# A selective scan, attention and routed experts in one kernel: disjoint scatter views, sums on TensorE, one table set, a new order of partitions, and an earlier gather

## The chip, the cores and the metric

The kernel runs on one core of a Trainium2 chip. All data is float32. The metric is the device time of one execution in microseconds (us). Before the change the median of three runs is 3942.65 us (3942.25 to 3942.79).

A core has five engines that run their own instruction streams in order and wait for each other by semaphores: PE (TensorE: weight load and matmul), DVE (VectorE), ACT (ScalarE), POOL (GpSimd) and SP (which here only issues DMAs). Sixteen DMA engines move data between DRAM and the on-chip memory, whose 128 partitions are its rows.

## The reference

The input `x` is (4, 384, 32, 32): four images, 384 channels, 1024 positions. Cut to what matters:

```python
# layer 0: four directions k; state size 16; each (image, k, channel, state) is a recurrence over 1024 positions
x_dbl = einsum('bkdl,kcd->bkcl', cross_scan(groupnorm(x)), x_proj_weight)
dts, Bs, Cs = split(x_dbl)                         # 12, 16, 16 rows
dt = softplus(einsum('bkrl,kdr->bkdl', dts, dt_projs_weight) + dt_projs_bias)
h = h * exp(dt * A) + (dt * u) * B                 # step by step over l
y = sum over the 16 states of h * C  (+ D * u)
x = x + gelu(layernorm(merge of the four directions of y))
# layer 1, on tokens t = x as (4, 1024, 384)
t = t + causal_attention(layernorm(t))             # one head of width 384
g = top 2 of softmax(layernorm(t) @ gate_w)        # 4 experts, renormalised
t = t + sum over the 2 of g_e * (gelu(ln(t) @ w1[e] + b1[e]) @ w2[e] + b2[e])   # 384 -> 1536 -> 384
```

## The kernel before, in words

**Units and ticks.** The scan is cut into 768 units (192 per image). A unit is 32 channels times 4 states, which fill the 128 partitions, times 1024 positions. A Python loop over ticks `t` writes out the order of the instructions for every engine: one unit a tick, and beside it pieces of all other work, which are generators that yield "wait n ticks" or "this took PE about n us". So the order within each engine is fixed when the kernel is built.

**One unit.** `decay` (ACT, L606): `da = exp(dt * a)`. `front` (DVE, L613): `v = du * B` into PSUM. `middle` (DVE, L619): the recurrence as one scan instruction. `back` (POOL, L636): `h * C`, ordered to run beside the scan of the next unit. After four units `row` (PE, L661) sums the four states of each channel with the 0/1 matrix `sel` and adds into `y`. `ahead` makes DVE wait, once the first image is done, until buffers that it will need are free: there are 7 buffers of `h`.

**The order of partitions.** Partition p holds channel p // 4 and state p % 4 of its unit. Hence three broadcast loads, all issued by SP: `dt` and `du` (`spread_dt`, L574) read 32 rows of DRAM, each for 4 partitions in a row; `bc` (`spread_bc`, L585, once for B and once for C) reads 4 rows, the four of them 32 times over. Each is 128 rows of 4096 bytes.

```python
src = dts_d[u["b"], u["k"]][which, g * DJ : (g + 1) * DJ, :]
src = bass.AP(tensor=src.tensor, offset=src.offset, ap=[src.ap[0], [0, NI], src.ap[1]])   # dt, du
src = bass.AP(tensor=src.tensor, offset=src.offset, ap=[[0, DJ], *src.ap])                # bc
```

An `ap` lists [step, count] from the slowest dimension to the fastest; NI is 4, DJ is 32. `dt` is fetched 5 ticks ahead of its unit, `du` and `bc` 3 ticks. `dt` and `du` have four buffers each and serve 16 units (four groups of states); `bc` has two buffers, each for four units.

**The first image** has no attention or experts beside it. For part of its units `feed` and `turned` make `v` on ACT (L901) and PE (L923) in place of DVE: 104 of the 192.

**Softplus.** `project_dt` (once for each of 6 parts of an image) computes `dt` with two Exp and two Ln on ACT (L448, L450), and one tick later DVE bounds it (`bounded`, L454) and multiplies (L491). Exp and Ln are in different table sets of ACT, so each change costs an ACT_TABLE_LOAD.

**Routing and experts.** After attention each image's 1024 tokens go through `ready` in two halves of 4 chunks of 128 tokens: gates, top 2, and a place for each token in the lists of its two experts. Then 8 indirect DMAs a half, issued by POOL (L1319), scatter the token rows into `xs_d`. All write to the one tensor `xs_d`, so each waits for the one before it to land. `experts` runs 11 blocks of 256 tokens (L1483: 384 to 1536, L1521: 1536 to 384) with weights loaded by SP (L1416), and stores into `ys_d`. `combine` and `joined` gather each token's two rows (POOL, L1562), scale and add them on DVE (L1577), add the bias term by a small matmul and DVE (L1582, L1585), turn the result on PE (L1590) and store it.

**What overlaps.** Attention, routing and experts of image b run beside the scan of image b + 1. The last image's run alone after the last unit (the tail).

Of the kernel before, what the change touches and what calls it, by code (L numbers as in the profile page):

```python
# [16 lines left out]
P = 128  # L17
B = 4
# [36 lines left out]
def hybrid_kernel(  # L55
# [67 lines left out]
    class Shared:  # L123
# [24 lines left out]
    banks = Shared(  # L148
        FIRST_BANKS,
        lambda i, name: (ps_m if i < FIRST_BANKS else pools["pm"]).tile(  # L150
            [P, 512], F32, tag=f"pm{i}", name=name
        ),
        0,
    )
# [4 lines left out]
    def bank(name):  # L159

        ps = banks.now(name)
        banks.give(name)
        return ps

# [11 lines left out]
    ys_d = [dram.tile([E * CAP, C], F32, tag=f"ys_{i}", name=f"ysd_{i}") for i in range(1)]  # L176
    g_d = dram.tile([P, M, C], F32, tag="g", name="g_d")
# [17 lines left out]
    for i in range(NI):  # L195
        nc.scalar.dma_start(a_raw[i::NI], a_logs.rearrange("(g d) n -> d g n", d=DJ))
# [27 lines left out]
    state_i = const.tile([P, NI], F32, tag="state_i", name="state_i")  # L224
# [8 lines left out]
    dump = const.tile([P, 1], F32, tag="dump", name="dump")  # L233
# [10 lines left out]
    fresh = const.tile([P, E, 4], F32, tag="fresh", name="fresh")  # L244
    nc.gpsimd.memset(fresh, 1.0)
    nc.gpsimd.memset(fresh[:, :, 0:1], 0.0)
# [8 lines left out]
    nc.scalar.activation(a_raw, a_raw, AF.Exp)  # L255
    nc.scalar.activation(dump, eps, AF.Sqrt)

    def scan_weights():
        nc.vector.tensor_reduce(state_i, ident.rearrange("p (d i) -> p i d", i=NI), AX.X, ALU.add)
        nc.vector.tensor_scalar_mul(state_i, state_i, -1.0)  # L260
        nc.vector.memset(a4, 0.0)
        for i in range(NI):
            nc.vector.scalar_tensor_tensor(
                a4, a_raw.rearrange("p g (q i) -> p g q i", i=NI)[:, :, :, i],
                state_i[:, i : i + 1], a4, ALU.mult, ALU.add,
            )
        nc.vector.tensor_reduce(sel, ident.rearrange("p (d i) -> p d i", i=NI), AX.X, ALU.add)
# [90 lines left out]
    def groupnorm(b, u):  # L358
# [3 lines left out]
        if b > 0:  # L362
            var_c = sm.tile([P, M], F32, tag="gn_vc", name=f"gn_vc_{b}")
            sq = yield from slots.take(f"gn_sq_{b}", P, L)
            for m in range(M):
                nc.scalar.activation(
                    sq, u[m], AF.Identity, scale=-1.0 / L, accum_out=mean_c[:, m : m + 1]
                )
                yield "wait", 1
            for m in range(M):  # L370
                nc.scalar.activation(
                    sq, u[m], AF.Square, bias=mean_c[:, m : m + 1], accum_out=var_c[:, m : m + 1]
                )
                yield "wait", 1
# [26 lines left out]
        nc.scalar.activation(rstd, ps, AF.Sqrt, bias=eps)  # L401
# [4 lines left out]
        for m in range(M):  # L406
# [4 lines left out]
            else:  # L411
                nc.scalar.activation(
# [32 lines left out]
    def softplus(xs, logs):  # L445

        for x_, log in zip(xs, logs):
            nc.scalar.activation(log, x_, AF.Exp)  # L448
        for log in logs:
            nc.scalar.activation(log, log, AF.Ln, bias=1.0)  # L450
# [5 lines left out]
    def project_dt(b, pair, m, u, xd):  # L456
# [12 lines left out]
        for h in range(NH):  # L469
# [12 lines left out]
            for i, k in enumerate(ks):  # L482
                nc.scalar.activation(
# [4 lines left out]
        yield "wait", 1  # L488
# [15 lines left out]
    def first_dt(u, xd):  # L504
# [9 lines left out]
        for (i, h), ps in pss.items():  # L514
            nc.scalar.activation(
                dts[i][:, bass.ts(h, 512)], ps, AF.Identity, bias=dtb[:, ks[i], 0:1]
            )
# [17 lines left out]
    def preparation(b):  # L535
# [8 lines left out]
        if b == 0:  # L544
            nc.scalar.activation(dump, eps, AF.Exp)
# [21 lines left out]
    def spread_dt(n, which, tag):  # L567
# [5 lines left out]
        src = bass.AP(tensor=src.tensor, offset=src.offset, ap=[src.ap[0], [0, NI], src.ap[1]])  # L573
# [4 lines left out]
    def spread_bc(n):  # L578
# [3 lines left out]
        for j in range(2):  # L582
            src = rows_d[u["b"], u["pair"]][u["i"], j, u["q"] * NI : (u["q"] + 1) * NI, :]
            src = bass.AP(tensor=src.tensor, offset=src.offset, ap=[[0, DJ], *src.ap])
# [17 lines left out]
    def decay(n):  # L602
# [3 lines left out]
        u["decay"] = nc.scalar.activation(  # L606
# [84 lines left out]
    def layernorm(dst, src, name, lag):  # L691
# [29 lines left out]
        for h in range(n):  # L721
            for c in range(M):
                s = bass.ts(h, 512)
                nc.scalar.activation(sqs[c][:, s], dst[:, c, s], AF.Square)
# [14 lines left out]
        nc.scalar.activation(  # L739
# [28 lines left out]
    def fold():  # L768
# [36 lines left out]
        for m in range(M):  # L805
# [7 lines left out]
            nc.scalar.activation(g[:, m, :], ps[:, :C], AF.Copy, scale=-scale)  # L813
# [25 lines left out]
    def feed():  # L839
# [21 lines left out]
        for n in range(0, IMAGE, EACH):  # L861
# [19 lines left out]
            for q in range(NQ):  # L881
                n0 = n + q * NJ
                if n0 // NJ % 5 not in (1, 3, 4) or clock[0] > n0 - AHEAD:
# [9 lines left out]
                for h in range(2):  # L893
# [5 lines left out]
                    for t in range(4):  # L899
                        for i in range(NI):  # L900
                            nc.scalar.activation(  # L901
                                st[:, 4 * h + t, :].rearrange("p (d i) -> p i d", i=NI)[:, i, :],
                                ps[h][:, t * P : (t + 1) * P], AF.Copy,
# [25 lines left out]
    def finish(b):  # L929
# [8 lines left out]
        for m in range(M):  # L938
            nc.scalar.activation(
# [11 lines left out]
    def scaled_tokens(b, yb):  # L951

        sqs = []
        for c in range(M):
            sq = yield from slots.take(f"sq_at_{b}_{c}", P, L)
            nc.scalar.activation(sq, yb[:, c, :], AF.Square)
# [17 lines left out]
        nc.scalar.activation(flat, var[:, NH * P : 2 * NH * P], AF.Square)  # L974
# [3 lines left out]
        nc.scalar.activation(rs, rs, AF.Sqrt, bias=eps)  # L978
# [28 lines left out]
    def attention(b, yb, fx0):  # L1007
# [66 lines left out]
        def softmax(i, ss, pr):  # L1074
# [8 lines left out]
            for n, (o, e, ps) in enumerate(ss):  # L1083
                nc.scalar.activation(  # L1084
# [6 lines left out]
        def normalise(i, nb, n):  # L1091
# [4 lines left out]
            nc.scalar.activation(prs[i][:, :wd], prs[i][:, :wd], AF.Copy, scale=nb[:, 2:3])  # L1096

        def turn(i):
# [14 lines left out]
            slots.give(f"pr_{b}_{i}")  # L1113

        moments = sm.tile([P, NB, 2], F32, tag="moments", name=f"moments_{b}")

        def values(i):
# [14 lines left out]
            def rows():  # L1132
# [8 lines left out]
                if i % 4 == 3:  # L1141
                    h = i // 4
                    if h == 1:
                        rt = routes[b] = Route(b)
                    rows_ = fx0 if h == 0 else routes[b].rows
                    defer(1, lambda: side.append(ready(b, h, yb, rows_, moments)))
# [22 lines left out]

    def ready(b, h, yb, rows, moments):  # L1170

        name = f"{b}_{h}"
        mean, rstd = moments[:, 4 * h : 4 * h + 4, 0], sm.tile([P, 4], F32, tag="rstd", name=f"rstd_{name}")
        shift = sm.tile([P, 4], F32, tag="shift", name=f"shift_{name}")
        nc.scalar.activation(rstd, moments[:, 4 * h : 4 * h + 4, 1], AF.Sqrt, bias=eps)
# [4 lines left out]
        chunks = [yb[:, :, bass.ts(4 * h + q, P)] for q in range(4)]  # L1180
        xts = []
        for q in range(4):
            nc.scalar.activation(
                rows[:, q, :].rearrange("p (m t) -> p m t", m=M), chunks[q], AF.Identity,
                bias=shift[:, q : q + 1], scale=rstd[:, q : q + 1],
# [3 lines left out]
        if h == 1:  # L1189
            held.clear()  # L1190
        pg = yield from banks.take(f"pgate_{name}")
        for q in range(4):
# [7 lines left out]
            yield "pe", 0.5  # L1200
            yield "wait", 1
            nc.scalar.copy(xt[:, q % 2, :], ps[:, :C])
            banks.give(f"pxt_{name}_{q}")
            xts.append(xt[:, q % 2, :])
        yield "wait", 1
        for q in range(4):
# [5 lines left out]
        yield "pe", 2.6  # L1212
        slots.give(f"xt_{name}_0", f"xt_{name}_2")
        yield "wait", 1
        sc = sm.tile([P, 4, E], F32, tag="sc", name=f"sc_{name}")
        nc.vector.tensor_tensor(
            sc, pg[:, : 4 * E].rearrange("p (q e) -> p q e", e=E),
            gb.unsqueeze(1).to_broadcast([P, 4, E]), ALU.add,
# [4 lines left out]
        def over(v):  # L1223
            return v.unsqueeze(2).to_broadcast([P, 4, E])

        red = sm.tile([P, 4], F32, tag="red", name=f"red_{name}")
        nc.vector.tensor_reduce(red, sc, AX.X, ALU.max)
        nc.vector.tensor_tensor(sc, sc, over(red), ALU.subtract)
        nc.scalar.activation(sc, sc, AF.Exp)
# [4 lines left out]

        cmp = [one.tile([P, 4, E, E], F32, tag=f"cmp{i}", name=f"cmp{i}_{name}") for i in range(2)]
        each = sc.unsqueeze(3).to_broadcast([P, 4, E, E])
        other = sc.unsqueeze(2).to_broadcast([P, 4, E, E])
# [3 lines left out]
            cmp[1], cmp[1], lower.unsqueeze(1).to_broadcast([P, 4, E, E]), ALU.mult  # L1241
        )
        nc.vector.tensor_tensor(cmp[0], cmp[0], cmp[1], ALU.max)
        cnt = sm.tile([P, 4, E], F32, tag="cnt", name=f"cnt_{name}")
        nc.vector.tensor_reduce(cnt, cmp[0], AX.X, ALU.add)

        sel = sm.tile([P, E, 4], F32, tag="sel", name=f"sel_{name}")
        nc.vector.tensor_single_scalar(sel.rearrange("p e q -> p q e"), cnt, 1.5, ALU.is_lt)
        cum = sm.tile([P, E, 4], F32, tag="cum", name=f"cum_{name}")
        nc.vector.tensor_tensor_scan(  # L1250
            cum.rearrange("p e q -> p (e q)"), fresh.rearrange("p e q -> p (e q)"),
# [3 lines left out]
        mk = sm.tile([P, 4, E], F32, tag="mk", name=f"mk_{name}")  # L1255
        nc.vector.scalar_tensor_tensor(mk, cnt, 1.5, sc, ALU.is_lt, ALU.mult)
        nc.vector.tensor_reduce(red, mk, AX.X, ALU.add)
        nc.vector.tensor_scalar_add(red, red, 1e-9)
        nc.vector.reciprocal(red, red)
        nc.vector.tensor_tensor(mk, mk, over(red), ALU.mult)  # L1260

        counts[b, h] = cum
        pp = yield from banks.take(f"place_{name}")
        flat = pp[:, : 4 * E]
# [6 lines left out]
        if h == 1:  # L1271
            before = counts[b, 0][:, :, 3:4]
            nc.tensor.matmul(
                flat.rearrange("p (e q) -> p e q", e=E), ones, before.to_broadcast([P, E, 4]),
                start=False, stop=True,
            )
            for i in range(2):
                nc.tensor.matmul(
                    pp[:, 4 * E : 5 * E], ones, counts[b, i][:, :, 3], start=(i == 0), stop=(i == 1)
                )  # L1280
        yield "pe", 1.5
        pm = yield from banks.take(f"pm_{name}")
        for q in range(4):
            nc.tensor.transpose(pm[:E, q * P : (q + 1) * P], mk[:, q, :], ident)
        yield "pe", 0.5
# [6 lines left out]
        at = sm.tile([P, E, 4], F32, tag="at", name=f"at_{name}")  # L1292
        nc.vector.tensor_tensor(at, flat.rearrange("p (e q) -> p e q", e=E), base, ALU.add)
        spot = sm.tile([P, 4, 2], F32, tag="spot", name=f"spot_{name}")
        two = [sm.tile([P, E, 4], F32, tag=f"two{i}", name=f"two{i}_{name}") for i in range(2)]
# [479 lines left out]
```

## Time and profile before

The profiled execution took 3944.32 us, and its span from first to last instruction is 3942.6 us.

| stretch of the span, us | what runs | DVE busy | PE busy | DMA share | GB/s |
|---|---|---|---|---|---|
| 0 to 50 | groupnorm and projections of image 0 | 18.0 | 20.3 | 0.61 | 174 |
| 50 to 750 | scan of image 0 | 605.2 | 418.8 | 0.60 | 215 |
| 750 to 1634 | scan of image 1 | 792.3 | 702.1 | 0.64 | 224 |
| 1634 to 2511 | scan of image 2 | 782.8 | 687.9 | 0.62 | 216 |
| 2511 to 3341 | scan of image 3 | 773.3 | 661.7 | 0.60 | 209 |
| 3341 to 3488 | tail: layer norm, attention | 45.6 | 129.2 | 0.16 | 49 |
| 3488 to 3551 | tail: routing and scatters | 12.1 | 15.3 | 0.24 | 80 |
| 3551 to 3902 | tail: experts | 0.0 | 350.7 | 0.53 | 167 |
| 3902 to 3943 | tail: gathers, sums, stores | 14.0 | 19.4 | 0.56 | 164 |

Busy columns are microseconds within the stretch. The DMA share is the mean busy share of the 16 DMA engines. In the four scan stretches DVE is busy 86 to 93% of the time; in the last stretches other engines set the end.

### The profile page before, as it was taken

How to read it: one execution, taken by the hardware profiler on the slowest of the kernel's cores; microseconds unless marked ns; L12 is line 12 of the kernel's file. 1: busy time of each engine (PE TensorE's matmuls, PEld its weight loads, DVE VectorE, ACT ScalarE, POOL GpSimd, SP SyncE). 2: the span in 40 equal slices, each digit the busy share in tenths (PEclk: the TensorE clock that was granted, in tenths of full speed). 3: DMA queues.
4: the chain of work that ended last, by engine and by line, in shares of the span. 5: the costliest groups of instructions: out<-in, count | busy, mean ns of one | idle time of the engine just before them, and what ended most of it. 6: DMA issues, size and time to landing. Idle time of an engine off the chain costs nothing. (4 is left out here: it accounts for less than half of the span.)

```text
span 3942.6 us, 40290 instructions
## 1 busy us (share of the span) xinstructions
PE 3005.2 (76%) x12787; PEld 1745.6 (44%) x12787; DVE 3043.2 (77%) x2250; ACT 2093.9 (53%) x3244; POOL 1973.9 (50%) x929
## 2 busy tenths in 40 slices
PE   4566655779478889678559799678479997859997
PEld 1233333335145556234235566234146663537774
DVE  5888888999988888989898899999889999310001
ACT  5778888556465567346446566255245553322211
POOL 2576666645565555645554566755565666010001
PEclk7677777789689999789669999779589998869998
DMA  5557655454467778534457878543368876115554
GB/s 190 195 206 262 240 197 194 173 190 165 146 215 277 277 251 307 192 137 169 145 198 252 300 247 304 190 162 136 112 222 311 279 276 208 50 52 180 180 174 139
DMA packets 405154, 798.17 MB, mean 202 GB/s; under 512 B 47484, under 2 KB 278572, under 8 KB 404940
## 3 DMA queue, kind: packets, MB, share of 16 engines
q1 hardware_dynamic: 390540, 770.01, 56.2%
q0 software_dynamic: 8192, 25.17, 1.9%
q8 instruction: 102, 1.67, 0.2%
q10 hardware_dynamic: 6208, 0.39, 0.1%
q14 instruction: 112, 0.92, 0.1%
HBM read 680.44 MB, written 115.02 MB: 202 GB/s over the span
## 5 line engine op out<-in xcount | busy, mean ns | idle before, releaser
L636 POOL TENSOR_TENSOR h<-h,bc 128x1024 f32<-128x1024 f32 x768 | 1814.9, 2369 | 1306.9 <-DVE v L613 1146.0
L619 DVE TENSOR_TENSOR_SCAN h<-da,v 128x1024 f32<-128x1024 f32 x768 | 1748.9, 2283 | 49.7 <-PE v L923 18.0
L606 ACT ACTIVATE da<-dt,a 128x1024 f32<-128x1024 f32 x768 | 884.2, 1159 | 777.4 <-DVE h L619 668.5
L613 DVE TENSOR_TENSOR v<-du,bc 128x1024 f32<-128x1024 f32 x664 | 888.9, 1339 | 181.1 <-PE y L661 66.2
L661 PE MATMUL y<-h,sel 128*32 128x512 f32 x3072 | 612.3, 716 | 281.1 <-POOL h L636 271.8
L1483 PE MATMUL ph<-turned,w 128*128 128x256 f32 x3168 | 733.8, 390 | 83.9 <-DMA w<-in_w 81.5
L1521 PE MATMUL py<-w,ht 128*128 128x384 f32 x2112 | 702.6, 490 | 14.7 <-DMA w<-in_w 14.3
L1483 PEld LDWEIGHTS ph<-turned,w 128*128 128x128 f32 x3168 | 611.5, 196 | 213.2 <-issue 89.2
L1521 PEld LDWEIGHTS py<-w,ht 128*128 128x128 f32 x2112 | 398.2, 191 | 314.8 <-issue 31.6
L1491 ACT ACTIVATE ht<-ph,b1t 128x256 f32<-128x256 f32 x528 | 221.1, 470 | 590.4 <-PE ph L1483 551.0
L661 PEld LDWEIGHTS y<-h,sel 128*32 128x32 f32 x3072 | 108.2, 121 | 657.2 <-POOL h L636 427.0
L1577 DVE SCALAR_TENSOR_TENSOR z<-g,shares,z 128x384 f32<-128x384 f32 x64 | 60.8, 951 | 409.3 <-DMA g<-ysd,places 408.4
L1562 POOL DMA_INDIRECT g<-ysd,places x64 | 73.5, 1148 | 394.4 <-DMA z<-t2d 368.1
L923 PE MATMUL v<-ident,st 128*128 128x128 f32 x832 | 152.9, 346 | 145.9 <-DVE h L619 145.2
L901 ACT ACTIVATE st<-turn,bt 128x128 f32<-128x128 f32 x832 | 242.7, 544 | 0.1
L923 PEld LDWEIGHTS v<-ident,st 128*128 128x128 f32 x832 | 125.5, 180 | 186.3 <-DVE h L619 105.7
L1319 POOL DMA_INDIRECT xsd<-fx,places x32 | 39.7, 1240 | 204.8 <-ACT mt L1311 143.7
L454 DVE SCALAR_TENSOR_TENSOR dt<-du,dt 128x1024 f32<-128x1024 f32 x48 | 64.3, 1339 | 77.9 <-ACT du L450 68.3
L1126 PE MATMUL po<-vt,pt 128*128 128x384 f32 x288 | 110.0, 532 | 13.4 <-ACT pt L1024 13.3
L475 PE MATMUL pdt<-xd,wdt 12*128 12x512 f32 x184 | 86.5, 806 | 34.7 <-ACT st L901 13.9
L1449 PE MATMUL pxg<-ident,xg 128*128 128x128 f32 x264 | 40.0, 290 | 84.7 <-DMA xg<-xsd 84.7
L1063 PE MATMUL ss<-axn,qt 128*128 128x512 f32 (+3 forms) x288 | 101.2, 496 | 4.2 <-ACT pr L1084 3.2
(263 smaller groups left out, 2316.4 us busy)
## 6 DMA issues: line engine op xcount, KB each, us to landing
w<-in_w SPq DMA_DIRECT2D x528, 384.0 KB
bc<-rows SPq DMA_DIRECT2D x384, 512.0 KB
dt<-dts SPq DMA_DIRECT2D x192, 512.0 KB
du<-dts SPq DMA_DIRECT2D x192, 512.0 KB
dts<-dt SPq DMA_DIRECT2D x48, 512.0 KB
dts<-du SPq DMA_DIRECT2D x48, 512.0 KB
xg<-xsd SPq DMA_DIRECT2D x44, 384.0 KB
ysd<-yt SPq DMA_DIRECT2D x44, 384.0 KB
```

The lines of the kernel that those rows point to most:

```text
L606: u["decay"] = nc.scalar.activation(u["da"], spread["dt4", n], AF.Exp, scale=a4[:, g, u["q"] : u["q"] + 1])
L613: return nc.vector.tensor_tensor(u["v"], spread["du4", n], spread["bc", n][:, 0, :], ALU.mult)
L619: nc.vector.tensor_tensor_scan(u["h"][:, ::step], u["da"][:, ::step], u["v"][:, ::step], 0.0, op0=ALU.mult, op1=ALU.add,)
L636: product = units[n]["product"] = nc.gpsimd.tensor_tensor(h, h, spread["bc", n][:, 1, :], ALU.mult)
L661: units[n]["row"] = nc.tensor.matmul(y, sel, h, start=first, stop=last, tile_position=(0, jj * DJ))
L901: nc.scalar.activation(st[:, 4 * h + t, :].rearrange("p (d i) -> p i d", i=NI)[:, i, :], ps[h][:, t * P : (t + 1) * P], AF.Copy, scale=bt[ ...
L923: nc.tensor.transpose(u["v"][:, t * P : (t + 1) * P], st[:, t, u["j"] * P : (u["j"] + 1) * P], ident)
L1063: nc.tensor.matmul(ps[:, : e - o], qt[:, c, i * P : (i + 1) * P], xn[o // 512][:, c, : e - o], start=(c == 0), stop=(c == M - 1 and (alone ...
L1126: nc.tensor.matmul(po[:, :C], pts[i][:, j, :], vt[:, j, :], start=False, stop=(j == i))
L1483: nc.tensor.matmul(ps[:, i * BT : (i + 1) * BT], t[:, c, i * P : (i + 1) * P], xt[:, c, :], start=(c == 0), stop=(c == M - 1),)
L1491: nc.scalar.activation(ht[:, f + i, :], ps[:, i * BT : (i + 1) * BT], AF.Gelu if alone else AF.Identity, bias=biases[j][:, f + i : f + i + 1],
L1521: nc.tensor.matmul(pss[i][:, :C], hts[j][:, 2 * c + f, i * P : (i + 1) * P], t[:, f, :], start=(c == 0 and f == 0), stop=(c == 5 and f == 1),)
```

## The change

Five things are changed together.

1. **Scatters.** `dram_disjoint_views(xs_d[0], 16)` makes 16 views of the list tensor that are declared not to overlap; each scatter of an image writes through its own. The routing goes in three groups of 4, 2 and 2 chunks in place of two halves. In the last image no ticks lie between the scatters of a group.
2. **Sums.** `combine` no longer uses DVE: for each chunk ACT builds two diagonal matrices from the token's shares, and 12 matmuls of 128x128 add the residual, the bias term and the two scaled rows, already turned, in one PSUM tile.
3. **Tables.** All ACT functions go through `act`, which loads the set `natural_log_exp_and_others` for Exp and Ln alike. `project_dt` waits two ticks in place of one before DVE bounds the result.
4. **States 32 partitions apart.** Partition p now holds state p // 32 and channel p % 32. The broadcast loads, `a_raw`, `a4`, `sel` and the writes of `st` follow. `feed` asks for other units (three groups of four in place of three of five), of which 91 of 192 are made.
5. **The end.** For the last image the gather of each token's first row is issued after the last block but one (`early`), the second after the last block (`late`); four more PSUM tiles serve the tail (`more_banks`), and DVE copies half of each `yt`.

```diff
+    views = dram_disjoint_views(xs_d[0], 2 * L // P)
...
+    def act(dst, src, f, **more):
+        if f in KINDS:
+            tables_for(KINDS[f])
+        return nc.scalar.activation(dst, src, f, **more)
...
-        yield "wait", 1
+        yield "wait", 2
         for i, k in enumerate(ks):
             bounded(dts[i], dus[i])
...
-        src = bass.AP(tensor=src.tensor, offset=src.offset, ap=[src.ap[0], [0, NI], src.ap[1]])
+        src = bass.AP(tensor=src.tensor, offset=src.offset, ap=[[0, NI], *src.ap])
         nc.sync.dma_start(t, src)
...
-            src = bass.AP(tensor=src.tensor, offset=src.offset, ap=[[0, DJ], *src.ap])
+            src = bass.AP(tensor=src.tensor, offset=src.offset, ap=[src.ap[0], [0, DJ], src.ap[1]])
             nc.sync.dma_start(bc[:, j, :], src)
...
-                if n0 // NJ % 5 not in (1, 3, 4) or clock[0] > n0 - AHEAD:
+                if n0 // NJ % 4 == 0 or clock[0] > n0 - AHEAD:
                     continue
...
+    GROUPS = ((0, 4), (4, 2), (6, 2))
...
                 nc.gpsimd.indirect_dma_start(
-                    out=xs_d[0],
+                    out=views[2 * (q0 + q) + i],
...
+    def add_up(ps, g, z, terms, first, last):
+        for n, what in enumerate(terms):
+            for m in range(M):
+                s = bass.ts(m, P)
+                lhs, rhs = {
+                    "t2": (z[:, s], ident),
+                    "b2": (b2s[:, s], g[:E, 2 * C : 2 * C + P]),
+                    0: (g[:, m * P : (m + 1) * P], z[:, 2 * C : 2 * C + P]),
+                    1: (g[:, C + m * P : C + (m + 1) * P], z[:, 2 * C + P : 2 * C + 2 * P]),
+                }[what]
+                nc.tensor.matmul(ps[:, s], lhs, rhs, ...)
...
+    def early(b):
+        for i in range(L // P):
...
+            gather(b, i, g, 0)
+            beside(b, i, g, z)
+        yield "wait", 3
+        for i in range(L // P):
+            ps = yield from banks.take(f"pz_{b}_{i}")
+            add_up(ps, *closing[i], ("t2", "b2", 0), True, False)
...
+    def late(b):
+        for i in range(L // P):
+            gather(b, i, closing[i][0], 1)
+        for i in range(L // P):
...
+            add_up(ps, g, z, (1,), False, True)
+            put_out(b, i, ps, z)
```

## The prediction

> **What bounds the kernel now.** I read the windows by stage first (the table above), then the groups of instructions, then the waits, then the chain that ended last. The groups name the engine that bounds the scan:
>
> ```profile
> L636 POOL TENSOR_TENSOR h<-h,bc 128x1024 f32<-128x1024 f32 x768 | 1814.9, 2369 | 1306.9 <-DVE v L613 1146.0
> L619 DVE TENSOR_TENSOR_SCAN h<-da,v 128x1024 f32<-128x1024 f32 x768 | 1748.9, 2283 | 49.7 <-PE v L923 18.0
> L613 DVE TENSOR_TENSOR v<-du,bc 128x1024 f32<-128x1024 f32 x664 | 888.9, 1339 | 181.1 <-PE y L661 66.2
> ```
>
> POOL's 1146 us of idle time are spent waiting for DVE's `v`; DVE's scan has 49.7 us of idle time before it in all. So DVE sets the pace: a tick on DVE is 2.283 + 1.339 = 3.62 us (2.3 where `v` comes from ACT and PE), and 768 ticks fill 3291 us (50 to 3341), 4.3 us each. After 3341 the chain runs through PE, the scatters and the gathers. DVE's waits:
>
> ```profile
> DVE z L1577 <- DMA g<-ysd,places: 408.4, 9, 397.0
> DVE dt L454 <- ACT du L450: 68.3, 16, 7.3
> DVE v L613 <- PE y L661: 66.2, 26, 11.8
> DVE v L613 <- DMA du<-dts: 43.6, 24, 5.3
> DVE v L613 <- DMA bc<-rows: 18.9, 11, 4.8
> ```
>
> The first is the idle tail. DMA costs DVE some 62 us today, in 35 waits: the engines keep up. That depends on what part 4 of the change touches:
>
> ```profile
> q1 hardware_dynamic: 390540, 770.01, 56.2%
> ...
> bc<-rows SPq DMA_DIRECT2D x384, 512.0 KB
> dt<-dts SPq DMA_DIRECT2D x192, 512.0 KB
> du<-dts SPq DMA_DIRECT2D x192, 512.0 KB
> ```
>
> 768 broadcast loads of 128 rows of 4096 bytes are 402.7 of the 770 MB, all on SP's one queue.
>
> **Part 4, the order of partitions: the term that decides.** The loads keep their bytes and packets; the slowest dimension of the source falls from 32 to 4 (dt, du: 4 copies of 32 rows; bc: 4 rows of 32 copies). The trace has no such load of 4096-byte rows, but its semaphore records show how transfers are shared out: every load of 128 rows or 32 x 4 raises its semaphore in 16 updates; `wdt` loads of 12 rows give 13 (12 and one more), and `z<-gtd`, `gtd<-mt`, `b2s`, whose slowest dimension is 4 rows, give 5 (4 and one). So I read that a transfer whose slowest dimension counts 4 runs on 4 engines of the 16. The built instruction of the changed kernel still carries [32, 4] in this order.
>
> [...] The rows show the counts; which four engines, no run here shows. [...]
>
> Price, from the packet records: the 118,912 packets of 4096 bytes take 159 ns in the median and 181 ns in the mean (a tenth over 191). Now each of 16 engines has 8 packets of a load (1.3 to 1.4 us); on four, each has 32: 5.09 to 5.79 us a load. Identical shapes should make an identical choice, so I take the same four each time: 768 x 5.09 to 5.79 = 3908 to 4448 us on each, mid 4178. Their other work: the DMA share times the length of the four stretches is 0.60 x 700 + 0.64 x 884 + 0.62 x 877 + 0.60 x 830 = 2027 us per engine, of which the loads are 768 x 8 x 0.181 = 1112; 915 stay. So the four engines need 4823 to 5363 us for a scan that takes 3291, mid 5093: 6.6 us a tick against DVE's 3.62. I add 60 us (bounds 0 and 400): `dt` and `du` have four buffers each, freed only four ticks before the next group needs them, so 10 of the 16 loads of every 16 units fall into some five ticks, while in the others the loads can wait for buffers. Scan: about 5150 in place of 3291. If the four varied from load to load, two or three loads would share the 16 engines, only the delay to landing would grow (1.3 to 5.4 us, against a lead of 3 to 5 ticks, 11 us or more), and this term would be 0 to +200.
>
> Small: 26 groups of turned units become 23, 13 units more at 1.256 us (median of `v`): +16 on DVE. All that is below the DMA floor; it counts only if the loads stay fast.
>
> **Part 1, scatters.** At the end 16 stand in a row:
>
> ```profile
> 3534.36 0.96 POOL L1319 DMA_INDIRECT xsd<-rows,places  x1 [1.87 <-DMA xsd<-rows,places]
> 3537.69 0.96 POOL L1319 DMA_INDIRECT xsd<-rows,places  x1 [2.37 <-DMA xsd<-rows,places]
> 3540.52 0.96 POOL L1319 DMA_INDIRECT xsd<-rows,places  x1 [1.88 <-DMA xsd<-rows,places]
> ...
> 3912.72 0.95 POOL L1562 DMA_INDIRECT g<-ysd,places  x1 [0.30 <-issue]
> 3913.97 0.95 POOL L1562 DMA_INDIRECT g<-ysd,places  x1 [0.30 <-issue]
> ```
>
> A scatter comes every 3.08 us, 0.96 of it issuing, the rest the landing of the one before. The gathers, which wait for none, come every 1.25 us. First issue 3494.5, last landing 3543.1; the last places are known at 3509.2, after which 4 scatters (the last group's) need 5 us and a landing of 2.6, or 8 need 10: ready at 3517 to 3521 with some microseconds for the third group's own routing: -23 (bounds -26 and -15). Beside the scan (images 0 to 2) POOL stalls in its wait, `back` is late behind it, `h` and `y` come late and DVE waits. `v` took 888.9 us where 664 medians of 1.256 would be 834: 55 stretched; with the waits for `y` and `sc` beside scatters the six windows hold 78 us over their ticks. I take -60 (bounds -78 and 0, the latter if POOL's issuing, 2 x 1.25 a tick beside 2.36 of `back`, is what delays it).
>
> **Part 2, sums.** These two DVE rows go:
>
> ```profile
> L1577 DVE SCALAR_TENSOR_TENSOR z<-g,shares,z 128x384 f32<-128x384 f32 x64 | 60.8, 951 | 409.3 <-DMA g<-ysd,places 408.4
> L1585 DVE TENSOR_TENSOR z<-z,pb 128x384 f32<-128x384 f32 x32 | 17.2, 538 | 8.2 <-PE pb L1582 7.5
> ```
>
> 78 us, of which 14 in the last stretch and the rest (some 60) on DVE in the scan: -57. PE gets 12 matmuls for 4, the extra 8 at about 0.29 us (`pxg`, 128x128: 290 ns), 2.3 us for 24 chunks: 55 us, laid on PE's idle time (168 us or more in each stretch from 750 on); uncovered it is +55. ACT builds 64 diagonals at 0.3 to 0.5 us, beside 380 idle us a stretch.
>
> **Part 3, tables.** `bounded` no longer stands at DVE's head waiting for Ln: 68.3 us in 16 waits, 4.3 each. One table load less (24 at L450, 1.283 us each) and a tick more of lead: -55 (bounds -68, and -20 if only the load time is saved). The later `dt` is due several ticks on.
>
> **Third routing group.** 36 small DVE instructions of about 0.2 us, three images: +21.
>
> **Part 5, the end.** From the last `py` (3901.7) to 3942.6 are 41 us: 16 gathers in 20, then sums, turning, stores. Eight gathers fewer (10 us) and no DVE sums: -15 (bounds -17, and -12 if the store of block 10 waits for the early gathers, 2.7). Prologue: two table loads, -2.
>
> **Sum.** On the profiled execution's span, 3942.6 (1.7 us lie around it; the median is 3942.65, so no correction): prologue 48 + scan 5150 + tail 602 - 38 = 5762. Predicted: 5750. Bounds of the terms: 4823 to 5763 for the scan, plus 612: about 5430 to 6380; a four-engine share a little smaller than the median packet's gives 5300. Own range 5300 to 6300.
>
> **Rivals.**
> - *The loads stay on 16 engines* (the share-out isn't by the slowest dimension, and the five updates of 4-row transfers come from their being 4 rows in all, on both sides). For it: in those rows both sides are short, in the new loads the destination has 128 partitions. Then only the gains count: -60 -57 -55 +16 +21 -23 -15 -2 = -175: 3768 (3700 to 3860). Chance 0.15.
> - *Four engines, varying.* Against it: nothing in the trace suggests a rotation. +80 on the last: about 3850 (3770 to 4050). Chance 0.08; 0.06 of it faster.
> - *The queue couples* (the other side, beyond the forecast): SP issues everything in order, and an expert's weights (528 loads of 384 KB) or `xg` stand behind broadcasts that wait for buffers; the in-order PE then waits at L1483 with `y` behind it, and DVE for `y`. It decides if weights land over 10 us late in many blocks: 33 blocks x 12 loads x 2 to 3 us is 800 to 1200 on top: 6300 to 7200. Against it: `w` is waited for only 14 times now, 81.5 us. Chance 0.08.
> - *The views don't loosen the scatters*: a variant of any case, 80 us more, within its range.
>
> **How the numbers follow.** The forecast (same four engines) has 0.69. A measurement tells 0.2%, 8 us, from no change. Faster: 0.15 + 0.06 = 0.21; same 0.01; slower 0.78. The range must take in the fast cases to leave out no more than 2 in 10: 3720 to 6350, beside the forecast's own 5300 to 6300.
>
> **What would show it.** Right: scan ticks of 6.5 us or more from image 0 on; a DMA share near 0.4 and some 140 GB/s there with four engines full; DVE at L613 and ACT at L606 waiting for `du`, `bc`, `dt` at the top of the waits; five updates per broadcast load; DVE busy near 55%. Parts 1 to 3 and 5: scatters 1.25 us apart; no waits at L454's line; no DVE sums; 3488 to 3551 some 23 us shorter, the end 15 shorter. Wrong: a scan of 3300 us or less with 16 updates a load, or ticks that differ from image to image by what the experts load.

## The result, and the profile after

The changed kernel takes 5948.4 us (median of 4 runs, 5942.3 to 5958.6), the kernel before 3942.7 us: a ratio of 1.508 [1.505, 1.511]. The profiled execution took 5947.4 us, its span is 5945.6 us.

The windows of the four scan stretches (images 0 to 3) of the changed kernel. Columns: length, busy us of PE, weight load, DVE, ACT, POOL with instruction counts, granted clock, DMA share, GB/s.

```profile
66.00:1202.00 1136.00, 442.94 (x1814) 193.11 (x1814) 632.49 (x348) 503.62 (x1047) 456.92 (x192) 0.62 0.34 129
1202.00:2590.00 1388.00, 799.31 (x3064) 453.84 (x3064) 780.71 (x604) 497.46 (x642) 482.00 (x214) 0.75 0.43 143
2590.00:3997.00 1407.00, 791.30 (x3014) 456.57 (x3014) 779.59 (x580) 464.97 (x599) 494.87 (x224) 0.74 0.42 135
3997.00:5343.00 1346.00, 775.03 (x2990) 456.02 (x2991) 751.66 (x552) 413.59 (x540) 491.98 (x223) 0.74 0.41 130
```

The scan lasts 5277 us in place of 3287 (first scan instruction to last), while DVE's busy time in it is the same as before (2944 us against 2954): it is busy 56% of the time, not 90. The loss is waiting. Data moves at 129 to 143 GB/s and the 16 DMA engines are busy 34 to 43% of the time on average, where 60 to 64% was common: the loads are slower and yet the engines are idler. A tick takes 5.9 us in image 0 and 7.0 to 7.3 us in images 1 to 3.

The waits of the changed kernel, largest first (total us, times, longest):

```profile
ACT da L192 <- DMA dt<-dts: 1049.2, 132, 23.5
DVE v L640 <- DMA bc<-rows: 981.1, 103, 24.0
DVE v L640 <- DMA du<-dts: 867.1, 131, 21.8
...
PE py L1583 <- DMA w<-in_w: 488.2, 75, 23.9
PE ph L1545 <- DMA w<-in_w: 472.9, 65, 29.6
...
DVE v L640 <- PE y L688: 255.1, 55, 16.0
```

DVE's waits at `v` for `du` and `bc` were 62 us and are 1848. ACT waits 1049 us for `dt`. PE's waits for weights, which share SP's queue with the broadcasts, grew from some 96 us to 961. DVE's timeline at the start of a group of 16 units (start, length, instruction, idle time before it and its releaser) shows the pace of the loads:

```profile
290.52 1.23 DVE L640 TENSOR_TENSOR v<-du,bc 128x1024 f32<-128x1024 f32 x1 [9.10 <-DMA du<-dts]
291.89 2.29 DVE L646 TENSOR_TENSOR_SCAN h<-da,v 128x1024 f32<-128x1024 f32 x1
295.61 1.23 DVE L640 TENSOR_TENSOR v<-du,bc 128x1024 f32<-128x1024 f32 x1 [1.43 <-DMA du<-dts]
296.97 2.29 DVE L646 TENSOR_TENSOR_SCAN h<-da,v 128x1024 f32<-128x1024 f32 x1
300.68 1.23 DVE L640 TENSOR_TENSOR v<-du,bc 128x1024 f32<-128x1024 f32 x1 [1.42 <-DMA du<-dts]
```

Here one `du` lands every 5.08 us, which is 32 packets of 159 ns on one engine (the 4096-byte packets around it take 160 to 162 ns in the median). Loads that stood on different engines would overlap here; these stand in one row. In the semaphore records every one of the 768 broadcast loads now gives 5 updates, and every other transfer what it gave before. The packet records agree: during the scan exactly four packets of 4096 bytes are in flight for 64% of the time, where the kernel before has exactly four for 1% and 16 or 17 for a quarter.

### The profile page after: what moved, and what is told of

Read it like the earlier page. It is cut to its first block, busy times and chain, and to the rows that moved or that the text cites. A ratio compares the mean times of both kernels' runs of the same rounds, so it can differ in the third digit from the quotient of the medians.

```text
span 5945.6 us, 41311 instructions
## 1 busy us (share of the span) xinstructions
PE 3367.7 (57%) x13307; PEld 1958.7 (33%) x13307; DVE 3022.0 (51%) x2307; ACT 2044.4 (34%) x3172; POOL 1975.4 (33%) x931
## 5 line engine op out<-in xcount | busy, mean ns | idle before, releaser
L1583 PE MATMUL py<-w,ht 128*128 128x384 f32 x1800 | 757.3, 575 | 492.5 <-DMA w<-in_w 488.2
L688 PE MATMUL y<-h,sel 128*32 128x512 f32 x3072 | 647.7, 740 | 465.6 <-POOL h L663 462.9
L1545 PEld LDWEIGHTS ph<-turned,w 128*128 128x128 f32 x2784 | 594.7, 218 | 641.6 <-issue 489.8
L192 ACT ACTIVATE ht<-ph,b1t 128x256 f32<-128x256 f32 x464 | 194.5, 471 | 910.9 <-PE ph L1545 841.7
L953 PE MATMUL v<-ident,st 128*128 128x128 f32 x728 | 136.6, 351 | 271.3 <-DVE h L646 244.0
L953 PEld LDWEIGHTS v<-ident,st 128*128 128x128 f32 x728 | 109.8, 181 | 323.8 <-DVE h L646 280.0
L192 ACT ACTIVATE st<-turn,bt 128x128 f32<-128x128 f32 x736 | 199.9, 391 | 7.8 <-PE turn L905 7.7
L1652 PE MATMUL pz<-ident,z 128*128 128x128 f32 x156 | 34.5, 380 | 205.6 <-DMA z<-t2d 177.2
L1164 PE MATMUL po<-vt,pt 128*128 128x384 f32 x234 | 93.1, 549 | 28.8 <-ACT pt L1054 28.8
L1652 PEld LDWEIGHTS pz<-ident,z 128*128 128x128 f32 x156 | 29.5, 275 | 221.5 <-issue 98.6
```

The source lines that it names most:

```text
L192: return nc.scalar.activation(dst, src, f, **more)
L688: units[n]["row"] = nc.tensor.matmul(y, sel, h, start=first, stop=last, tile_position=(0, jj * DJ))
L953: nc.tensor.transpose(u["v"][:, t * P : (t + 1) * P], st[:, t, u["j"] * P : (u["j"] + 1) * P], ident)
L1164: nc.tensor.matmul(po[:, :C], pts[i][:, j, :], vt[:, j, :], start=False, stop=(j == i))
L1545: nc.tensor.matmul(ps[:, i * BT : (i + 1) * BT], t[:, c, i * P : (i + 1) * P], xt[:, c, :], start=(c == 0), stop=(c == M - 1),)
L1583: nc.tensor.matmul(pss[i][:, :C], hts[j][:, 2 * c + f, i * P : (i + 1) * P], t[:, f, :], start=(c == 0 and f == 0), stop=(c == 5 and f == 1),)
```

## The experiments

**Undo part 4 alone** (e1), on the changed kernel. `sel`, `a4`, `a_raw` and the writes of `st` go back with the loads; the choice of turned units stays as changed. Cut to the loads:

```diff
-        src = bass.AP(tensor=src.tensor, offset=src.offset, ap=[[0, NI], *src.ap])
+        src = bass.AP(tensor=src.tensor, offset=src.offset, ap=[src.ap[0], [0, NI], src.ap[1]])
...
-            src = bass.AP(tensor=src.tensor, offset=src.offset, ap=[src.ap[0], [0, DJ], src.ap[1]])
+            src = bass.AP(tensor=src.tensor, offset=src.offset, ap=[[0, DJ], *src.ap])
```

> The changed kernel with part 4 undone: the channel-major order of partitions, its loads (slowest dimension 32), sel, a4 and the writes of st as before; parts 1, 2, 3 and 5 and the choice of turned units stay. Four-engine theory: the whole loss is the loads', so this gives what the prediction's first rival summed for the other parts, 3768 us (3700 to 3860), with 16 semaphore updates a load and a DMA share of 0.6 or more in the scan. Rival (another part, for instance the sums on PE, the third routing group or SP's order, holds the scan up): it stays above 3960 us.

Measured: 3811.5 us, 0.967 [0.965, 0.968] of the kernel before. The windows of this kernel, images 1 and 2:

```profile
734.00:1573.00 839.00, 708.25 (x3070) 415.44 (x3069) 776.00 (x606) 494.33 (x643) 483.42 (x214) 0.88 0.67 236
1573.00:2414.00 841.00, 701.37 (x3042) 408.18 (x3041) 771.93 (x579) 462.24 (x599) 497.70 (x224) 0.88 0.65 227
```

The same DVE work as above fits into 839 us in place of 1388, at a DMA share of 0.67, with 16 updates a load. So part 4 cost 2137 us, and the other parts together gain 131.

**Part 4 alone on the kernel before** (e2): the mirror of that edit.

> The kernel before with part 4 alone (partition order, loads with slowest dimension 4, sel, a4, st; not the choice of turned units). Four-engine theory: the scan is as long as in the changed kernel and the tail as before, 5948 + 38 for the tail's lost gains, so about 5990 us (5900 to 6100), 5 updates a load. Rival (the loss needs the other parts too): under 5000 us.

Measured: 5913 us (one run), inside the range, and again 5 updates for every broadcast load. Nothing else is needed for the loss.

**Two loads of 64 partitions in place of one of 128** (e3), on the changed kernel; bc likewise. The slowest dimension is now 2.

```diff
-        src = bass.AP(tensor=src.tensor, offset=src.offset, ap=[[0, NI], *src.ap])
-        nc.sync.dma_start(t, src)
+        src = bass.AP(tensor=src.tensor, offset=src.offset, ap=[[0, NI // 2], *src.ap])
+        for i in range(2):
+            nc.sync.dma_start(t[i * P // 2 : (i + 1) * P // 2], src)
```

> The changed kernel, each broadcast load issued as two of 64 partitions, slowest dimension 2. If a transfer with slowest dimension k always runs on the same k engines, both halves go to the same two: 64 packets per engine and load in place of 32, 768 x 32 x 0.159 to 0.176 us = 3908 to 4325 us more on them, so 9850 to 10300 us and 3 updates a half. Rival (the engines change from transfer to transfer): two halves cover four engines, no more than the changed kernel's 5950 us.

Measured: 9615 us (one run), 3 updates for every half. The two halves of a load could have used four engines between them; they use two: exactly two packets of 4096 bytes are in flight for 81% of the scan. So the halves, all of one shape, go to the same two. It is 235 us under my range: the 3667 us over the changed kernel are 149 ns for each of the 24,576 packets that each engine got on top, less than the 162 ns that a packet takes in the median of both kernels, so in the changed kernel the four engines can't have been full all the time. In 5% of its scan fewer than four packets of any size are in flight.

**Four loads of 32 partitions** (e4), the same edit with 4 in place of 2.

> The changed kernel, each broadcast load issued as four of 32 partitions: one copy of 32 rows (dt, du) or one row in 32 copies (bc), slowest dimension 32. The order of partitions stays. Four-engine theory: all 16 engines again, close to the run with part 4 undone, 3770 us; SP issues 3072 in place of 768, at about 0.57 us each 1750 us in a scan of 3100, so it has room, and the range is 3720 to 3950. Rival (the order of partitions itself costs, by sel, st or the pattern of DRAM rows): above 4500 us.

Measured: 4139 us, 1.049 [1.047, 1.051]. In the four scan stretches the DMA share is 0.73 to 0.76, where the changed kernel has 0.34 to 0.43: at 0.76 more than 12 of the 16 engines work on average. 1809 us come back with the new order of partitions kept, so these come from the loads' shape and not from the order. But 328 us are missing against e1, outside my range. DVE's waits for `du` are 196 us here, 44 in e1, and the queue line of the page shows slower transfers (packets, MB, share of 16 engines); e1's follows:

```profile
q1 hardware_dynamic: 427436, 770.16, 67.1%
```

```profile
q1 hardware_dynamic: 390572, 770.01, 57.7%
```

Within the span of e4 that is 2781 us per engine, against 2201 in e1, for the same bytes: a 4096-byte packet takes 249 ns in the median here, 159 in e1. Why the packets are slower was not tried: besides the 32 partitions of a transfer, their number (3072 in place of 768) and the order of partitions differ from e1 as well. So it is not shown that the 328 us are the packets' alone.

The remaining runs cut up the 131 us of e1, whose forecast was 175.

**Views undone** (e5), on e1: `out=xs_d[0]` in place of `out=views[...]`.

> The kernel of the run with part 4 undone (3811.5 us), part 1's views undone: all scatters write to xs_d[0] again; the three routing groups stay. By the prediction's terms +60 us in the scan (0 to 78) and +23 in the tail: 3894 us (3820 to 3915), scatters about 3.1 us apart. Rival (POOL's issuing, not the wait for landing, is what delays back): within 15 us of 3811 plus the tail's 23.

Measured: 3888.6 us, 77 more than e1 (in the profiled executions 53 in the scan and 22 in the tail). The scatters of e1 and then of e5 on POOL's timeline:

```profile
3386.96 0.98 POOL L1379 DMA_INDIRECT xsd<-fx,places  x1 [0.31 <-issue]
3388.24 0.96 POOL L1379 DMA_INDIRECT xsd<-fx,places  x1 [0.30 <-issue]
```

```profile
3444.31 0.96 POOL L1378 DMA_INDIRECT xsd<-fx,places  x1 [2.38 <-issue]
3447.15 0.96 POOL L1378 DMA_INDIRECT xsd<-fx,places  x1 [1.88 <-DMA xsd<-fx,places]
```

1.27 us apart with views, about 3.1 without: the views do what they say.

**Two table sets and one tick** (e6), on e1: the loads are left to the activations as before, and `yield "wait", 1` before `bounded`.

> The kernel of the run with part 4 undone (3811.5 us), part 3 undone: the table loads as before (Exp and Ln in different sets) and one tick between softplus and bounded. By the prediction's term +55 us (20 to 68): 3866 us (3830 to 3880), with the waits of DVE at bounded back at some 68 us. Rival (the stall is filled by later waits anyway): 3811 within 10 us.

Measured: 3906.2 us, above my range, 95 more than e1 (90 between the profiled executions: 71 in the scan, 17 in the tail, 2 ahead of the scan). ACT's group of table loads in e6, then in e1, and DVE's wait at `bounded` in e6, then in the scan of e1:

```profile
L191 ACT ACT_TABLE_LOAD x167 | 214.3, 1283 | 39.9 <-DMA wx<-in_w_x 14.4 <-DVE yb L790 8.3 <-DMA dt<-dts 6.8
```

```profile
L182 ACT ACT_TABLE_LOAD x122 | 156.5, 1283 | 12.5 <-issue 10.3
```

```profile
DVE dt L484 <- ACT du L191: 87.7, 21, 10.8
```

```profile
DVE dt L485 <- ACT du L192: 6.8, 7, 3.1
```

DVE's wait is back, 88 us of it, and with it 47 table loads of 1.28 us (two more stand on another line of e6): in e1 one set serves Exp and Ln. In the tail both kernels have 11 table loads. What differs there is that more of image 2's sums come after the scan in e6: 192 of their matmuls, the last ending 69 us after it, against 157 and 46 us. The sets and the tick were undone together; what each is worth alone was not tried.

**Sums on DVE again** (e7), on e1, for images 0 to 2: two scale-and-adds and one add on DVE, a bias matmul and three turning matmuls on PE.

> The kernel of the run with part 4 undone (3811.5 us), part 2 undone for images 0 to 2: two scale-and-add and one add on DVE, one bias matmul and three turning matmuls on PE. Two theories of what part 2 is worth: by the prediction's term the scan alone counts, +57 us, 3868. By the trace of that run, seven of image 2's eight chunks are summed on PE in the first 106 us of the tail, where PE has 28.3 us of them in place of some 8 before, and the attention there ends 22 us later: so the tail gives 20 back and the sum is about 3848 us (3830 to 3858).

Measured: 3824.0 us, 12.5 more than e1 (in the profiled executions 14 in the scan and 1 in the tail). Both of my theories fell. DVE's rows for the sums within the scan (instructions, busy us, mean ns):

```profile
L1660 DVE SCALAR_TENSOR_TENSOR z<-g,shares,z 128x384 f32<-128x384 f32 x32 | 25.1, 785 | 0.6
...
L1699 DVE TENSOR_TENSOR z<-z,pb 128x384 f32<-128x384 f32 x16 | 8.4, 528 | 0.0
```

Only 16 of the 24 chunks fall into the scan; image 2's come after its last unit. In the kernel before, whose chunks come one tick apart and not two, 19 did, with 52 us of DVE work. And the 33.5 us of DVE work here show as 17 us more busy time (2935.6 against 2918.7), since other instructions are less stretched: `v` takes 868 us, not 880. So e7 prices part 2 at the changed kernel's spacing of the chunks; at the old spacing it was not tried.

**No early gathers** (e8), on e1: the last image goes through `combine`.

> The kernel of the run with part 4 undone (3811.5 us), the early gathers of part 5 undone: the last image goes through combine as the others do, with its sums on PE. By the prediction's term (the early half is free beside block 10) the end grows by 15 us: 3826. By the trace, PE is busy for all of the experts' stretch, so the early matmuls push the last blocks back (311 us from first to last store in place of 296): 15 us come back there, and the end grows by some 4 to 16: 3800 to 3814 us.

Measured: 3824.8 us, 13 more than e1. The last blocks do finish earlier (304 us from first to last store, not 311), but the end after the last store grows from 29 to 51 us, more than I allowed. The prediction's 15 was near.

**Chunks of combine closer together** (e9), on e1: one tick apart in place of two.

> The kernel of the run with part 4 undone (3811.5 us), with combine's chunks one tick apart in place of two, and both gathers of a chunk in one tick, as in the kernel before. Theory: the last image's attention ends 22 us later after the scan than before the change because image 2's sums are spread over 21 ticks in place of 11 and run into the tail; closer together they leave it: attention 10 to 20 us shorter, about 3795 us (3788 to 3805). Rival (something else in the tail slows it, such as the four more PSUM tiles): 3811 within 6 us.

Measured: 3812.7 us, no difference from e1. All 24 chunks of images 0 to 2 now fall into the scan; in e1 it was some 17. The theory holds for the tail, which fell by 22 us: the first scatter comes 161 us after the last scan instruction, in e1 182. But the scan grew by 22, so what was taken out of the tail was paid there.

**No extra PSUM tiles in the tail** (e10), on e8: without

```diff
-        if t == NU + 4:
-            more_banks()
```

> The kernel of the run without the early gathers (3824.8 us), without the four more PSUM tiles in the tail. Theory (image 2's sums slow the tail's attention): no gain from it, 3825 us or up to 20 more, since the tail's work gets fewer PSUM tiles. Rival (two names share one tile of two banks, so that work on one half waits for the other): attention faster by 10 us or more, 3815 us or less.

Measured: 3791.9 us, 33 less than e8 (the tail of the profiled execution is 32.5 us shorter, its scan 2.4): attention ends 14 us earlier after the scan, the first expert tokens load 21 us earlier, the experts take 297 us, not 304, and the end after the last store 46, not 51. So the extra tiles cost 33 us: the time is the rival's. Image 2's sums are still in this tail (144 of their matmuls), and yet the first scatter comes 160 us after the last scan instruction, as early as in e9 (161), where the sums were gone and the tiles were there. So the delay of some 20 us needs both together: taking away either one takes it away. `y_end` and `v_end` are one tile for two names each. Some of PE's groups in the attention of the last image, e8 first, then e10:

```profile
L1161 PE MATMUL y_end<-ident,yb 128*128 128x128 f32 x18 | 3.4, 339 | 5.0 <-ACT pr L192 2.6 <-ACT pt L1055 2.4
...
L1137 PE MATMUL v_end<-ident,pr 128*128 128x128 f32 x5 | 1.1, 295 | 3.5 <-ACT yb L1175 1.8 <-ACT pr L192 1.7
```

```profile
L1161 PE MATMUL po<-ident,yb 128*128 128x128 f32 x48 | 7.4, 295 | 1.4 <-ACT xt L1251 1.4
L1137 PE MATMUL tp<-ident,pr 128*128 128x128 f32 x36 | 6.0, 293 | 0.0
```

In e8 a turning of `pr` into `v_end` waits for ACT's copy to `yb`, which reads `v_end`; in e10, without such tiles, that wait is gone. In these groups PE waits 8.5 us against 1.4, of the 33. The order in which PE gets the work changes with the number of tiles too; what the sharing of a tile and the order cost each stays open.

**The choice of turned units alone, on the kernel before** (e11):

> The kernel before with part 4's choice of turned units alone (three groups of four, 91 units in place of 104). The prediction's term: 13 units more for DVE at 1.256 us, +16 us, 3959 us. From the sum of the parts undone so far (scan: views 53, tables 73, sums 13 make 139, and the scan of that kernel is 133 shorter than before) the choice and the third routing group cost 6 us together: 3943 to 3949 us.

Measured: 3954.6 us against 3939.3, a ratio of 1.0047 [1.0030, 1.0064]: +15 us. The prediction's term (+16) holds, the residual of 6 that I had formed from undone parts does not; so these parts don't simply add up, by some 10 us.

**The parts that gain, put together** (e12): e10 with early gathers whose scaling and adding is done on DVE.

> What the runs point to, put together: the changed kernel with part 4's loads undone and without the four more PSUM tiles (3791.9 us with no early gathers), plus an early half that costs PE nothing: the first gather of each token is issued after the last block but one and scaled and added on DVE, which idles there; after the last block come 8 gathers, one scale-and-add on DVE and 6 matmuls a chunk. The end after the last store falls from 46 us to some 4 + 10 + 10 to 14 us, the experts stay at 297 us: 3771 us (3764 to 3780). Rival (what the early half saves is lost again, as with the early matmuls, 7.6 us in the experts): 3776 to 3792.

Measured: 3786.0 us, 0.959 [0.957, 0.961] of the kernel before (3945.9 us beside it): 160 us less. It lies in the rival's range, not in mine. Against e10 (0.963 [0.961, 0.964]) it is not clearly apart: the end after the last store fell from 46 to 34 us (I expected 24 to 28), and the experts took 300 us, not 297.

## Why the prediction was right, and where its terms were off

- **What bounds the kernel.** Right: DVE at 3.62 us a tick, with DMA keeping up. In e1, with fast loads, DVE is busy 2919 of the scan's 3156 us, 92%.
- **Part 4, four engines.** Right in mechanism and nearly in size. Five updates a load, 0.34 to 0.43 of DMA share, 129 to 143 GB/s, DVE 56% busy: all as named beforehand. That the engines are the same from load to load was the forecast's assumption, which no row of the kernel before showed. The runs show it: in the changed kernel a `du` lands every 5.08 us and exactly four packets of 4096 bytes are in flight for 64% of the scan, and in e3 exactly two for 81% of it, at 9615 us. Which numbers these engines have no run shows.
- **Part 4, the size.** The mean packet was 177 ns, so 768 x 32 x 0.177 = 4345 us of broadcasts on each of the four; with the 915 of other work that makes 5260, beside a scan of 5277. That this fits so closely is in part luck. The same sum for e3 is 768 x 64 x 0.169 + 915 = 9222 us, more than its scan of 8916, so 915 is too much for these engines, unless packets of one engine overlap in the records; and the changed kernel's were idle for part of the time, which the prediction had as 60 us of gaps. The two errors go against each other, and how large each is stays open.
- **The ticks.** Two of the recorded signs didn't come out as written. Image 0 has 5.9 us a tick, not 6.5 or more, and the ticks do differ between image 0 and the others (7.0 to 7.3), which the prediction counted as a sign against itself. Four engines fit that all the same. The broadcasts are 192 x 32 x 0.177 = 1087 us in every image. The rest of the DMA work, taken as spread evenly, is some 114 us an engine in image 0 (0.34 x 1136 less 272 of broadcasts) and 280 to 325 in the others. That makes 1201 us for image 0 and 1367 to 1412 for the others, beside stretches of 1136 and of 1346 to 1407 us. The prediction took one mean tick for all images.
- **The distance of 198 us** (5750 against 5948) is 131 in the scan (5281 up to the point to which I had counted 5150), 18 in the prologue (the first scan starts at 66 us, in e1 at 48), 34 in the tail, and what the forecast was rounded by. The range on record (3720 to 6350) is wide enough to hold the fast cases too; the four-engine case's own, 5300 to 6300, holds 5948 as well.
- **Part 1**: 60 and 23 forecast, 53 and 22 measured.
- **Part 2**: 57 forecast, 13 measured. The term that was mis-sized: I laid all DVE time outside the last stretch, some 60 us, on the scan's path. In the kernel before 52 of it lay there; at the changed kernel's spacing it is 33.5 (a third of the chunks run after the scan), and part of that only takes the place of stretching.
- **Part 3**: 55 forecast (20 to 68), 95 measured. Mis-sized the other way: I counted DVE's waits at `bounded`, which are 81 us apart between e6 and e1, and no gain in the tail, where 17 us were. There are as many table loads there in both, and more of image 2's sums in e6; that these make the 17 us was not tried.
- **Choice of turned units**: 16 forecast, 15 measured. The third routing group and DVE's half of the `yt` copies were not tried by themselves.
- **Part 5**: early gathers 15 forecast, 13 measured. But the four PSUM tiles, which I gave no cost and no gain, took 33 back. So the tail after the last scan instruction began is 602 us in the changed kernel and was 606 before: the scatters and the end gained some 36 us, and attention (first scatter 18 us later) and experts (312 us from first to last store, not 296) lost nearly as much.
- Sum of the gains: 3768 forecast, 3811.5 measured. Of the difference 44 are part 2, 33 the PSUM tiles, 8 part 1, and part 3's 40 go the other way. That the sum is only 43 off is luck, then: errors of 40 us and more cancel.
- **Rivals.** Loads on 16 engines, varying engines: refuted by the five updates and by e3. That the views would not loosen the scatters: refuted by e5. The coupling through SP's queue was there (PE waited 961 us for weights) but didn't decide: DVE's waits for `y` grew from 66 to 255 us, those for the loads to 1848, and the time stayed below the 6300 to 7200 of that rival. How much of the 255 is this coupling was not tried.

## What to carry to other kernels

A broadcast load lists its copies inside or outside the rows, depending on the order of partitions. Here the list with the small count outside gave 5 semaphore updates a load in place of 16 and exactly four packets of 4096 bytes in flight for 64% of the scan, and by itself it took the kernel from 3943 to 5913 us (e2). Read the number of semaphore updates of a few transfers in the trace before reordering partitions, and price a changed load per engine, not per byte. When bundling changes, undo each by itself: here one part cost 2137 us and hid a gain of 131, and inside that gain 33 us were lost to four more PSUM tiles in the tail. A saving on the bounding engine counts only for the stretch in which it bounds: check which chunks fall in that stretch, after the change as well as before.

## What was unexpected of the hardware

With loads of 32 partitions (e4, DMA share 0.73 to 0.76 in the scan) the 4096-byte packets take 249 ns in the median, with those of 128 partitions 159 ns (e1, 0.61 to 0.67), and with four or two engines at work 162 ns (the changed kernel, 5 updates a load, and e3, 3 updates a half). And PE's granted clock was lower where PE waited more: in images 1 to 3 it is 0.88 in e1, where PE is busy 83 to 85% of the time, and 0.74 to 0.75 in the changed kernel, where it is busy 56 to 58%. PE's busy time is 3061 us in e1 and 3368 us in the changed kernel for the same 13,307 matmuls. What sets the clock was not tried.
